# Phase 1 of a two-layer attention kernel: split float32r products in place of Strassen's seven

## The chip, the cores and the metric

The kernel runs on one core of one Trainium2 chip. The time is device microseconds for the whole kernel, from one launch. An "image" below is one of the eight entries of the batch.

## The reference

Two attention layers follow each other on x of shape (8, 512, 32, 32), that is 8 images of 512 channels and T = 1024 tokens. Only the first layer's projections matter here:

```
h   = group_norm(x)                       # 32 groups of 16 channels
qkv = einsum('oc,bct->bot', qkv_w, h) + qkv_b     # 1536 outputs from 512 channels
q, k, v = per head, fake_quant(each)      # needs min and max of all q, of all k, of all v
w   = softmax(q^T k * scale);  a = v w;  x = x + proj_w a + proj_b
# layer 1: group norm, q, k, v, softmax attention with one head, projection, residual
```

fake_quant uses the minimum and maximum over the whole tensor, so no score can be computed before all eight images have their q, k and v. This divides the kernel in two phases.

## The kernel before

**Phase 1** (the block that opens the pools p1w, p1, p1o and ps_1) computes q, k and v of all images, keeps running maxima and minima in columns of `rcs` and stores the raw values in DRAM (`q_d`, `k_d`, `v_d`). Then `ext`, `exa` and `scl` reduce the extremes to the three scales, and **phase 2** loads q, k and v, quantizes them and computes both attention layers. It takes the rest of the time, and the change leaves its code as it is.

In phase 1 the 512 channels lie on 128 partitions in CC = 4 chunks, and the 1024 tokens in two halves of 512. Three images of x are held (`p1`, tag x), loaded by `load_x` on SyncE's DMA queue. `norm_steps` takes statistics on VectorE, averages them over groups with two small matmuls on TensorE (`gps`, `gps2`), and scales x in place on VectorE.

Products are in full fp32. `qk_block(b, j)` computes q and k of a pair of heads for all tokens as one 2x2 by 2x2 block product with Strassen's seven products; `v_block(b, n)` does the same for v. The sums that Strassen needs are made on VectorE: `weight_sums` once, `token_sums` for each image. Each product is two accumulating matmuls of 512 columns (q, k) or four of 256 (v). `keep` copies intermediate sums out of PSUM on ScalarE, `add_max` adds and takes the maximum on VectorE, `store` takes the minimum and starts the DMA. For image 0, four of the twelve tiles of rows (q and k of the first pair) are plain fp32 products, because these can start as soon as a chunk of x is normed.

The order is written out by hand. Every block is a generator that yields after each product; the list TURNS says whose product is next, and a step of `ahead` (`prepare(b + 1)`, the next image's norm and token sums) is taken after every other product. `mm` keeps the matmuls in this order on TensorE. VectorE's instructions in phase 1 are put in order by the framework.

`l1p` is a pool whose tags (h, v, g, rs, rs1, acc1) are shared with phase 2's tiles. `load_folded` loads weights for phase 2 into tags h and v, on ScalarE's DMA queue.

Of the kernel before, what the change touches and what calls it, by code (L numbers as in the profile page):

```python
# [9 lines left out]
F32 = mybir.dt.float32  # L10
BF = mybir.dt.bfloat16
# [19 lines left out]
SM1 = 1.0 / math.sqrt(C)  # L31

# [21 lines left out]
def attn_pair_kernel(  # L54
# [145 lines left out]
    def mm(ps, lhsT, rhs, **kw):  # L200
        ins = nc.tensor.matmul(ps, lhsT=lhsT, rhs=rhs, **kw).ins  # L201
        part = lhsT.shape[-1] / P if lhsT.shape[-1] in (32, 64) else 1.0
        if rhs.dtype in (BF, F16):
            part *= 0.25 * lhsT.shape[0] / P
        pe.t += math.prod(rhs.shape[1:]) * 1.677e-3 * part
        if last_mm[0] is not None:
            tc.add_manual_dep(ins, last_mm[0].name, IN_ORDER, reason="order")
        last_mm[0] = ins
# [11 lines left out]
    def norm_steps(  # L220
        src, dst, wcol, bank, nm, ccs=range(CC), fine=False, put=None, mv=None
# [36 lines left out]
        )  # L258
        for hf in range(NH):
            for i, cc in enumerate(ccs):  # L260
                put(hf, 0.5, lambda i=i, cc=cc, hf=hf: dve.tensor_scalar(
                    dst(cc, hf), src(cc, hf), mean[:, i : i + 1], rstd[:, i : i + 1],
                    ALU.subtract, ALU.mult,
                ))
                if fine and i % 2 == 1:
                    yield
# [3 lines left out]
    def group_norm(src, dst, wcol, bank, nm):  # L270
        for _ in norm_steps(src, dst, wcol, bank, nm):
# [4 lines left out]
    q_d = [[dram.tile([P, T], F32, tag=f"q{b}_{j}", name=f"q_d{b}_{j}") for j in range(PAIRS)]  # L276
           for b in range(B)]
    k_d = [[dram.tile([P, T], F32, tag=f"k{b}_{j}", name=f"k_d{b}_{j}") for j in range(PAIRS)]
           for b in range(B)]
# [9 lines left out]
    with ExitStack() as fast:  # L289
# [84 lines left out]
        with tc.tile_pool(name="p1w", bufs=1) as p1w, tc.tile_pool(name="p1", bufs=3) as p1, tc.tile_pool(  # L374
            name="p1o", bufs=4
        ) as p1o, tc.tile_pool(name="ps_1", bufs=8, space=PSUM) as ps_1:
# [4 lines left out]
            wqkv = p1w.tile([P, CC, 3 * C], F32, name="wqkv")  # L381
            wn = {}
            xs, hs, cs = {}, {}, {}
            col = {n: 0 for n in ("qmax", "kmax", "vmax", "vmin")}

            def column(name, tile_):
                col[name] += 1
                return tile_[:, col[name] - 1 : col[name]]
# [7 lines left out]

            def load_x(b):
                xs[b] = p1.tile([P, CC, T], F32, tag="x", name=f"x1_{b}")
                for cc in range(CC):
                    nc.sync.dma_start(xs[b][:, cc, :], x_v[b, :, cc, :])  # L400
                    if b == 0:
                        nc.sync.dma_start(wqkv[:, cc, 0:C], w_qkv[:, cc, 0:C])

            def norm(b, parts=1, fine=False):

                hs[b] = xt = xs.pop(b)
                n = CC // parts
                return [
# [3 lines left out]
                        V_GN0W, one, f"a{b}_{i}", range(i * n, (i + 1) * n), fine,  # L412
                    )
                    for i in range(parts)
                ]

            K0, K1 = slice(0, CC // 2), slice(CC // 2, CC)

            room = l1p.tile([P, 6, 512], F32, tag="g", name="room")
            vs = room[:, 0:4, :].rearrange("p s (k n) -> p s k n", k=CC // 2)
            wa_flat = wa.rearrange("p s k n -> p (s k n)")
            ss = [
                wa_flat[:, i * 1024 : (i + 1) * 1024].rearrange("p (k n) -> p k n", k=CC // 2)
                for i in range(3)
            ] + [room[:, 4:6, :]]

            def tt_behind(*args):
                dve.tensor_tensor(*args)  # L430
                dve.after(normed)

            def weight_sums():
                tt = tt_behind
                (a11, a12), (a21, a22) = (
                    [wqkv[:, k, bass.ts(i, C)] for k in (K0, K1)] for i in (0, 1)
                )
                tt(ss[0], a21, a22, ALU.add)
                yield
                tt(ss[1], ss[0], a11, ALU.subtract)  # L440
                yield
                tt(ss[2], a11, a21, ALU.subtract)
                yield
                tt(ss[3], a12, ss[1], ALU.subtract)
                yield
                (w11, w12), (w21, w22) = (
                    [wqkv[:, k, 2 * C + i * C // 2 : 2 * C + (i + 1) * C // 2] for i in (0, 1)]
                    for k in (K0, K1)
                )
                tt(vs[:, 0], w11, w12, ALU.subtract)  # L450
                yield
                tt(vs[:, 1], w22, vs[:, 0], ALU.subtract)
                yield
                tt(vs[:, 2], w22, w12, ALU.add)
                yield
                tt(vs[:, 3], w21, vs[:, 1], ALU.subtract)
                yield

            def quarters(b):
                h = hs[b]  # L460
                return [h[:, k, bass.ts(hf, 512)] for k in (K0, K1) for hf in range(NH)]

            def token_sums(b):
                a, b_, c, d = quarters(b)
                cs[b] = t = l1p.tile(
                    [P, 4, CC // 2, 512], F32, tag="hv"[b % 2], name=f"sums_{b}"
                )
                tt = dve.tensor_tensor if b else tt_behind
                tt(t[:, 0], b_, a, ALU.subtract)
                yield  # L470
                tt(t[:, 1], d, t[:, 0], ALU.subtract)
                yield
                tt(t[:, 2], d, b_, ALU.subtract)
                yield
                tt(t[:, 3], c, t[:, 1], ALU.subtract)
                yield

            def prepare(b):
                yield from norm(b, fine=True)[0]
                yield from token_sums(b)  # L480

            def add_max(dst, ps, other, mx):
                dve.tensor_tensor_reduce(
                    dst, ps, other, 1.0, -3.0e38, ALU.add, ALU.max, accum_out=mx
                )

            def qk_block(b, j):

                a, _, c, d = quarters(b)
                t1, t2, t3, t4 = (cs[b][:, i] for i in range(4))  # L490
                a11, a12, a22 = wqkv[:, K0, 0:C], wqkv[:, K1, 0:C], wqkv[:, K1, C : 2 * C]
                s1, s2, s3, s4 = ss
                x, y = (one(f"qkps_{b}_{j}_{i}") for i in range(2))
                u = p1o.tile([P, 2, 512], F32, tag="u", bufs=2, name=f"u_{b}_{j}")
                u4 = p1o.tile([P, 512], F32, tag="u4", bufs=1, name=f"u4_{b}_{j}")
                q = p1o.tile([P, T], F32, tag="qk", name=f"q1_{b}_{j}")
                k = p1o.tile([P, T], F32, tag="qk", name=f"k1_{b}_{j}")
                bq, bk = qkb[:, j : j + 1], qkb[:, PAIRS + j : PAIRS + j + 1]

                def product(ps, w, r, start):  # L500
                    for i in range(CC // 2):
                        mm(
                            ps, lhsT=w[:, i, bass.ts(j, P)], rhs=r[:, i, :],
                            start=start and i == 0, stop=(i == CC // 2 - 1), skip_group_check=True,
                        )

                def keep(dst, bias):
                    act.activation(dst, x, AF.Identity, bias=bias)

                def store(t, mn, dst):  # L510
                    dve.tensor_reduce(
                        mn[:, b * PAIRS + j : b * PAIRS + j + 1], t, AX.X, ALU.min
                    )
                    nc.sync.dma_start(dst[b][j], t)

                product(x, a11, a, True)
                keep(u[:, 0, :], bq)
                yield
                product(y, a12, c, True)
                add_max(q[:, 0:512], y, u[:, 0, :], column("qmax", qmax))  # L520
                yield
                product(x, s2, t2, False)
                keep(u[:, 1, :], bk)
                yield
                product(y, s3, t3, True)
                yield
                product(x, s1, t1, False)
                keep(u4, bk)
                add_max(k[:, 512:T], y, u4, column("kmax", kmax))
                yield  # L530
                product(x, s4, d, False)
                dve.tensor_scalar(
                    q[:, 512:T], x, bq, None, ALU.add, ALU.max, accum_out=column("qmax", qmax)
                )
                store(q, qmin, q_d)
                yield
                product(y, a22, t4, False)
                add_max(k[:, 0:512], y, u[:, 1, :], column("kmax", kmax))
                store(k, kmin, k_d)
                yield  # L540

            def v_block(b, n):

                a, _, c, d = quarters(b)
# [1499 lines left out]
```

## Time and profile before

| | |
|---|---|
| median of 3 runs | 2645.51 us (2643.5 to 2645.55) |
| span of the profiled execution | 2641.2 us (no other time of that execution is given) |
| phase 1's last Strassen matmul ends | about 611.6 us into the span |
| TensorE busy in the span | 2585.6 us (98%) |
| VectorE busy | 1880.1 us (71%) |
| ScalarE busy | 1256.9 us (48%) |
| DMA, mean over the span | 92 GB/s |

PE is TensorE's matmul records, PEld its weight loads, which run beside them, DVE is VectorE, ACT ScalarE, POOL GpSimd, SP SyncE. A line such as `L201 PE MATMUL out<-in 128*128 128x512 f32 x8` is eight records, stationary tile 128*128, moving operand 128x512. Groups list busy time, mean ns of one record, and the engine's idle time ahead of it with its releaser. Matmul records are longer than their spacing, since they overlap.

### The profile page before, as it was taken

What the parts mean: (1) busy time and instruction counts of PE and PEld (TensorE: products, weight loads), DVE (VectorE), ACT (ScalarE), POOL (GpSimd) and SP (SyncE); (2) the same over time, 40 slices, a digit from 0 to 9 for tenths busy, and PEclk for the clock granted to TensorE, in tenths of its full rate; (3) what the DMA queues carried; (4) which work ended last, traced back from release to release, by engine and by line L of the source; (5) the groups of instructions that cost most, each with busy time, mean ns of one, the idle gap of its engine ahead of it and who ended that gap; (6) DMA issues with size and microseconds to landing.
All of it is one profiled execution on the core that took longest, in us unless ns stands there. A gap on an engine that the chain in (4) does not pass through costs nothing.

```text
span 2641.2 us, 33393 instructions
## 1 busy us (share of the span) xinstructions
PE 2585.6 (98%) x13150; PEld 1657.2 (63%) x13150; DVE 1880.1 (71%) x2733; ACT 1256.9 (48%) x1582; POOL 195.7 (7%) x157
## 2 busy tenths in 40 slices
PE   8999999998998999999999999999999999999998
PEld 4655555553235775766577567757665775677687
DVE  7766666658777777877777677778777776776544
ACT  0011111115866664666566566646665665664121
POOL 0000000001110001000100010011001000100000
PEclk9999999999999999999999999999999999999999
DMA  5233322234321132223222321322232123212211
GB/s 203 112 128 112 127 99 101 88 119 152 134 67 41 57 104 89 85 66 110 94 61 77 112 89 57 105 88 85 64 111 95 61 77 112 89 38 79 100 37 38
DMA packets 146887, 241.96 MB, mean 92 GB/s; under 512 B 26528, under 2 KB 92064, under 8 KB 145184
## 3 DMA queue, kind: packets, MB, share of 16 engines
q1 hardware_dynamic: 115872, 181.50, 20.5%
q10 hardware_dynamic: 30848, 58.23, 6.5%
q8 instruction: 105, 1.72, 0.3%
q14 instruction: 62, 0.51, 0.1%
HBM read 152.86 MB, written 86.28 MB: 91 GB/s over the span
## 4 chain that ended last, share of the span: by engine, by line
PE 83%; DVE 8%; ACT 3%; issue 2%; DMA 2%; POOL 1%; SPq 0%; ACTq 0%; DVEq 0%; POOLq 0%
PE s L201 15%; PE qkps L201 13%; PE o L201 12%; PE pj L201 8%; PE av L201 7%; PE v2ps L201 7%; PE vps L201 6%; PE g L201 5%; PE st L201 4%; PE sm L201 4%; ACT pt L86 2%; DVE two L86 1%; DVE sums L86 1%; DVE x L86 1%; DMA out_dram<-x 1%
## 5 line engine op out<-in xcount | busy, mean ns | idle before, releaser
L86 DVE TENSOR_TENSOR two<-pt,two 128x1024 f16<-128x1024 f32 x496 | 596.7, 1219 | 143.6 <-POOL two L909 114.1
L86 ACT ACTIVATE pt<-st,esc 128x1024 f32<-128x1024 f32 x496 | 527.0, 1116 | 355.3 <-PE st L201 335.5
L86 ACT CAST two<-pt 128x1024 f16<-128x1024 f32 x358 | 362.3, 1056 | 8.4 <-issue 5.8
L86 ACT ACTIVATE u<-qkps,qkb 128x512 f32<-128x512 f32 x90 | 61.9, 687 | 500.5 <-PE qkps L201 500.5
L909 POOL CAST two<-pt 128x1024 f16<-128x1024 f32 x128 | 171.0, 1336 | 1553.6 <-PE sm L201 1028.1
L201 PE MATMUL av<-two,v 128*64 128x512 f16 x1984 | 246.0, 383 | 0.0
L201 PE MATMUL s<-g,h 128*128 128x256 f32 x1024 | 234.1, 381 | 0.0
L201 PE MATMUL pj<-ao,wp 128*128 128x512 f32 x512 | 223.6, 595 | 0.0
L201 PEld LDWEIGHTS s<-g,h 128*128 128x128 f32 x1024 | 192.8, 190 | 31.9 <-issue 4.3
L201 PE MATMUL st<-q,k 64*128 64x512 bf16 x1024 | 162.0, 382 | 21.5 <-ACT pt L86 11.9
L201 PEld LDWEIGHTS <-v 128*64 128x64 f16 x1984 | 98.1, 109 | 133.5 <-issue 65.6
L201 PE MATMUL s<-g,sums 128*128 128x256 f32 x768 | 178.4, 381 | 0.2 <-DVE p L86 0.2
L201 PE MATMUL o<-p,v 128*128 128x256 f32 x768 | 175.2, 382 | 1.0 <-DVE p L86 1.0
L201 PEld LDWEIGHTS pj<-ao,wp 128*128 128x128 f32 x512 | 96.1, 190 | 121.3 <-issue 112.7
L201 PE MATMUL qkps<-sums,wa 128*128 128x512 f32 x360 | 164.6, 592 | 0.0
L201 PEld LDWEIGHTS o<-p,v 128*128 128x128 f32 x768 | 144.3, 190 | 27.1 <-issue 5.7
L201 PEld LDWEIGHTS s<-g,sums 128*128 128x128 f32 x768 | 144.7, 190 | 24.2 <-issue 4.1
L201 PE MATMUL qkps<-x,wqkv 128*128 128x512 f32 x304 | 141.1, 603 | 0.8 <-DVE x L86 0.8
L201 PE MATMUL sm<-two,ones 128*32 128x512 f16 x1984 | 137.7, 383 | 0.5 <-ACT rs L86 0.5
L201 PE MATMUL g<-h,wa 128*128 128x256 f32 x512 | 121.7, 386 | 2.1 <-DVE h L86 2.1
L201 PEld LDWEIGHTS <-k 64*128 64x128 bf16 x1024 | 33.9, 94 | 141.6 <-issue 139.1
L201 PE MATMUL v2ps<-wm,h 128*128 128x256 f32 x512 | 119.9, 383 | 0.7
(202 smaller groups left out, 3566.9 us busy)
## 6 DMA issues: line engine op xcount, KB each, us to landing
rs<-rs_d SPq DMA_DIRECT2D x80, 256.0 KB
x<-in_x_dram SPq DMA_DIRECT2D x32, 512.0 KB
raw<-q_d SPq DMA_DIRECT2D x32, 512.0 KB
raw<-k_d SPq DMA_DIRECT2D x32, 512.0 KB
v_d<-v SPq DMA_DIRECT2D x32, 512.0 KB
x_d<-h SPq DMA_DIRECT2D x64, 256.0 KB
x<-x_d ACTq DMA_DIRECT2D x64, 256.0 KB
out_dram<-x SPq DMA_DIRECT2D x64, 256.0 KB
```

The lines of the kernel that those rows point to most:

```text
L86: ins = self.latest = op(*args, **kw).ins
L201: ins = nc.tensor.matmul(ps, lhsT=lhsT, rhs=rhs, **kw).ins
L909: copy(two[:, 0], pt)
```

## The change

Phase 1 no longer uses Strassen's scheme. Each fp32 operand is split into a high and a low half of 12 bits each, both kept as float32r, and a third term `mix`. Of two split operands the four half products come out of three products: high by high and low by low are summed in one PSUM bank, a; the mixed term by the mixed term is summed in another, m; `put` combines the two with fixed factors.

- `split_weights` makes the three forms of the weights once (`wsp`: w_high, w_low, w_mix), in six chunks; `split_half(b, hf)` makes them for one half of one image's tokens. The high part and the scaled low part of the weights are made on ScalarE, low and mix on VectorE.
- `three` issues 8 matmuls into a and 4 into m for each 128x512 tile of output; for v a ninth matmul (`pick`, `vrow`) adds the bias into a.
- `put` copies a to SBUF on ScalarE with scale and bias (`u_ring`), then adds m on VectorE and takes the maximum. `store` takes the minimum over two tiles and starts one DMA of 512 KB.
- `apply` scales x by the norm on ScalarE, one instruction for each channel chunk, except for image 0.
- x lies in the tags h and v of `l1p` (two images), the split halves in p1 (two), q's and k's output in `out_ring` (the memory of wa, three tiles), v's in `v_ring` (three tiles).
- q and k lie in DRAM by two pairs of heads (`q_two`, `k_two`); q_d and k_d are views of these.
- Image 0 still computes q and k of its first pair in full fp32.
- The order is by halves: all blocks of the first token half of an image, then all of the second. Beside the blocks go the steps of `side`: in the first half the split of the image's second half and the norm of the next image, in the second half the next image's first split. `load_x(b + 2)` is issued at the start of the second half, `load_folded("v", ...)` in the last image's second half.

The core of the diff:

```diff
+            def split_weights(g, cs):
+                high, low, mix = (t[:, g, cs] for t in wsp)
+                act.activation(high, raw_w[:, g, cs], AF.Identity, scale=NUDGE)
+                dve.tensor_tensor(low, raw_w[:, g, cs], high.bitcast(F32), ALU.subtract)
+                dve.after(normed)
+                dve.scalar_tensor_tensor(
+                    mix, low.bitcast(F32), -SH, high.bitcast(F32), ALU.mult, ALU.add
+                )
+                dve.after(normed)
+                act.activation(low, low.bitcast(F32), AF.Identity, scale=SH)
+
+            def split_half(b, hf):
+                halves[b, hf] = t = p1.tile(
+                    [P, 3, CC, 512], F32R, tag="half", name=f"half_{b}_{hf}"
+                )
+                for k in (slice(0, CC // 2), slice(CC // 2, CC)):
+                    high, low, mix = (t[:, i, k, :] for i in range(3))
+                    src = xs[b][:, k, bass.ts(hf, 512)]
+                    act.activation(high, src, AF.Identity, scale=NUDGE)
+                    yield
+                    dve.tensor_tensor(low, src, high.bitcast(F32), ALU.subtract)
...
+                    dve.scalar_tensor_tensor(
+                        mix, low.bitcast(F32), -SH, high.bitcast(F32), ALU.mult, ALU.add
+                    )
...
+            def three(nm, left, right, first=None):
+                a, m = (one(f"{nm}_{i}") for i in range(2))
+                pairs = [(left[i][cc], right[i][cc]) for i in range(2) for cc in range(CC)]
+                if first is not None:
+                    pairs.insert(0, first)
+                for i, (lt, rt) in enumerate(pairs):
+                    mm(a, lhsT=lt, rhs=rt, start=(i == 0), stop=(i == len(pairs) - 1))
+                for cc in range(CC):
+                    mm(m, lhsT=left[2][cc], rhs=right[2][cc], start=(cc == 0), stop=(cc == CC - 1))
+                return a, m
+
+            def put(dst, a, m, bias, name):
+                i = turn_of("u", 3)
+                u = u_ring[:, i, :] if i < 2 else u_last
+                act.activation(u, a, AF.Identity, bias=bias, scale=-(SH + 1.0))
                 dve.tensor_tensor_reduce(
+                    dst, m, u, -1.0 / SH, -3.0e38, ALU.add, ALU.max, accum_out=column(name)
+                )
+
+            def store(t, name, dst):
+                dve.tensor_reduce(column(name), t, AX.XY, ALU.min)
+                nc.sync.dma_start(dst, t)
...
-            TURNS = (0, 0, 2, 0, 0, 2, 0, 2, 0, 0, 2, 1, 1, 2, 1, 1, 2, 1, 2, 1, 1)
...
+            for b in range(B):
+                for hf in range(NH):
+                    if hf == 0:
+                        ahead = norm(b + 1, fine=True)[0] if b + 1 < B else iter(())
+                        if b == 0:
+                            side = [more, more, ahead]
+                        else:
+                            side = [split_half(b, 1), ahead]
...
+                    for _ in blocks(b, hf):
+                        for g in side:
+                            go(g)
+                        n += 1
+                        if hf == 1 and b + 1 < B and n == (4 if b else 3):
+                            for _ in ahead:
+                                pass
+                            side = [split_half(b + 1, 0)]
```

For image 0, `more` is the first half's split, the six chunks of weights and the second half's split in turn.

## The prediction

> **What bounds the kernel now.** I start with the page's busy times, to see which engine could set the end, and then look at the change's own stage, phase 1, with busy time by stretch. The stretches begin where the timeline of TensorE (PE) shows the first Strassen block (51.83), the start of image 1 (about 99.8), image 7 (538.4) and the end of phase 1 (611.6).
> ```profile
> PE 2585.6 (98%) x13150; PEld 1657.2 (63%) x13150; DVE 1880.1 (71%) x2733; ACT 1256.9 (48%) x1582; POOL 195.7 (7%) x157
> 52.00:99.80 47.80, 47.80 (x169) 31.62 (x169) 38.50 (x80) 4.12 (x6) 1.02 (x1) 1.00 0.19 74
> 99.80:538.40 438.60, 437.68 (x1371) 257.89 (x1371) 287.82 (x565) 49.49 (x72) 6.05 (x6) 1.00 0.29 111
> 538.40:611.60 73.20, 73.13 (x227) 42.59 (x225) 39.08 (x79) 8.24 (x12) 0.00 (x0) 1.00 0.31 118
> ```
> After the stretch and its length come busy us of PE, PEld, DVE, ACT, POOL, then granted clock and DMA share. PE is busy for all but 1 us in 438.6, at full clock; VectorE (DVE) 66%, ScalarE (ACT) 11%. Busy alone isn't peak, so I check the cadence: in the chain of waits the same piece recurs once per image.
> ```profile
> 128.72 3.40 DVE sums L86 x3
> ...
> 201.82 3.40 DVE sums L86 x3
> ...
> 274.93 3.40 DVE sums L86 x3
> ```
> The period is 73.1 us. The timeline of 330 to 345 us shows what fills it:
> ```profile
> 331.85 1.89 PE L201 MATMUL vps<-room,sums 128*128 128x256 f32 x8
> 331.85 1.49 PEld L201 LDWEIGHTS vps<-room,sums 128*128 128x128 f32 x7 [0.24 <-issue]
> 333.57 1.88 PE L201 MATMUL qkps<-x,room 128*128 128x512 f32 x4
> ```
> Every fp32 matmul leaves two records (high and low part of the weights), so four matmuls are eight records. Eight of 256 columns take 333.57 - 331.85 = 1.72 us, 0.215 each; in the chain eight of 512 columns take 3.43, 0.429 each. An image has 4x14 matmuls of 512 columns and 2x7x4 of 256: 112 x 0.429 + 112 x 0.215 = 72.1 us of the 73.1. So PE streaming is the bound here, and the 1.0 left is the group norm's two small matmuls and rare waits.
>
> **What the Trainium skill says.** "TensorE: Matmul & The Clock Gate", section "Wait — 56ns, not 53.3ns?", gives N/2.4 GHz + 2.5 ns for a warm one-pass matmul, 216 ns at 512 columns. The same page, "LDWEIGHTS (loading the stationary operand)", prices a load by its 128 columns, an estimate of 107 ns; the records here are 190. "Perfetto Trace Analysis", section "Engine Utilization", halves the output rate for fp32's low/high form. The trace agrees: 256 columns twice in 0.215, 512 twice in 0.429. Its step ① ("Step-by-step: what each phase is for", first page) has loads pulled ahead of running matmuls: the seven loads above follow every 0.215 us, with no time added though each lasts 0.19. No page gives a speed for float32r.
>
> **PE's part.** A Strassen block goes; each output tile of 128x512 becomes 8 matmuls into a and 4 into m, with one more for v's bias. An image has 8 q, 8 k and 8 v tiles: 24 x 12 + 8 = 296 matmuls. Were float32r to stream one column per cycle, each would last 0.2155 (the page's 216, and the trace's 0.215 for equally long streams with equal loads): 63.8 us, against 72.1. The matmul is bounded below by that streaming. From above: were nothing hidden, 0.19 + 0.215 = 0.405; were float32r run like fp32, 0.86. I take the low end, because a 0.19 load under a 0.215 stream is what v's records show. With the same 0.9 for the norm an image is 64.7 us, 8.4 less than 73.1.
>
> **The vector engine's part** must stay below 64.7. Durations, from groups by shape within 99.8 to 611.6:
> ```profile
> L86 DVE CUSTOM_DVE_ANT_0 v<-vps,uv 128x512 f32<-128x512 f32 x43 | 29.6, 688 | 42.6 <-PE vps L201 42.3
> L86 DVE TENSOR_REDUCE rcs<-v 128x1 f32<-128x1024 f32 x29 | 35.3, 1219 | 0.8
> L86 DVE BATCH_NORM_STATS2 gst_a<-x 128x6 f32<-128x512 f32 x40 | 25.8, 678 | 8.5 <-DMA x<-in_x_dram 8.2
> L86 DVE TENSOR_TENSOR sums<-x,sums 128x1024 f32<-128x1024 f32 x12 | 14.6, 1220 | 0.0
> L86 ACT ACTIVATE u<-qkps,qkb 128x512 f32<-128x512 f32 x84 | 57.7, 687 | 456.6 <-PE qkps L201 456.6
> ```
> Per image: 24 put (0.69 plus 0.08 accumulator read) 18.5; 12 minima 14.6; 8 statistics 5.4, 4 aggregates 0.8 and the small norm steps 1.2; four low of split_half at 1.22, 4.9; four mix. No immediate-scalar operation of mix's kind and size is shown; between 1.22 (as a tensor_tensor) and 1.42 (as ao's, 1416 ns with a pointer scalar) I take 1.3: 5.2. Sum 50.6 us, 78% of 64.7. The normalization leaves DVE for ACT.
>
> ACT: 24 x 0.69 for u, four high and four apply at about 1.1 (the exp of 128x1024 is 1116 ns): 16.5 + 8.9 = 25.4, under 40%. Both costs lie beside PE.
>
> **DMA and order.** Bytes are unchanged: 2 MB in, 6 MB out an image. The 12 stores stay 12 of 512 KB; q's and k's rows become 2 KB. 8.4 MB in 64.7 us is 130 GB/s, where the page's first slice moved 203. An x load now starts only when split_half(b, 1) has read that buffer, about mid-image, and the statistics need it half an image later: about 30 us for 2 MB; at 130 GB/s beside the stores it needs 16. SP's queue holds stores behind those loads; three-deep rings give a store over 10 us, so I cost it zero; without cover it would show as DVE waiting on q_d stores. load_folded("v") moves half an image forward on ACT's queue: two 1 MB issues, some 1.5 us of ACTq; no gain counted.
>
> **What gets a new wait.** In the first half of images 1 to 6 the norm's matmuls stand in PE's order, behind which every later tile is queued. They wait for statistics that share DVE with put and split_half. Over the first five tiles (13 us of PE) DVE has 5 x 0.77 + 2 x 1.22 + 1.22 x 2 + 1.3 + 6.2 = 16.2, so up to about 3 us of lag, or nothing if the statistics run ahead. They do run ahead in the old trace: fold_room, written after the whole loop, runs at 600.99 between phase 1's own evictions, so DVE's order follows readiness. I take 1.0 per image.
>
> **Image 0** keeps its 16 matmuls of q and k in full fp32 and must also split the weights. Its remaining PE work is 8 x 12 x 0.2155 + 8 x 13 x 0.2155 = 43.1 us, where 51.83 to 100.49 was 48.7: 5.6 gained at best. But DVE from 26.4 us has six weight chunks (2.52 each, 15.1), three half splits (5.04 each, 15.1), 8 evictions (6.7), 12 minima (14.6), the norm (7.4), 16 put (12.3) and about 2 for v's bias: 73 us by durations. In the old timeline 1.22-long records start every 1.13 (26.39, 27.53, 28.66), so some 100 of them overlap by 0.08 each: about 65 us net, for the 68 until 94.8. That is nearly full, so I leave only 1.5 of the 5.6.
>
> **Sum.** Image 0: 1.5; images 1 to 6: 6 x (8.4 - 1.0) = 44.4; image 7 without a norm: 8.4. Together 54.3. The end of phase 1 (last tile, minimum, partition reduction) is as long as before, and phase 2 is unchanged: zero, within 2 either way as its start shifts. The profiled span is 2641.2; no separate time of that execution is shown, and the median of the runs, 2645.5, lies 4.3 above it. 2641.2 - 54.3 + 4.3 = 2591.2.
>
> **Rivals.**
> (1) The weight load or the stream of float32r costs more than 0.244 us a matmul: (73.1 - 0.9)/296 is where the gain ends. For it: the trace has no float32r, and the margin is 13%. At 0.405 an image is 120.8 and the kernel 8 x 47 = 376 slower, 3020; run as fp32, worse (some 3700). If float32r isn't one pass the change doesn't do what it says, and it ends here too. Against: the 256-column cadence. Chance 0.10.
> (2) DVE lag becomes PE's wait: 3 us in six images and no gain in image 0 leave 6 x 5.4 + 8.4 = 41, less 3 for a late split: 38, 2607. For: 16.2 in 13 us. Against: readiness order. Chance 0.22.
> (3) Everything hides: 5.6 + 7 x 8.4 = 64, 2581. Chance 0.17.
> (4) Waits of several kinds (ring, x load, splits at image borders) eat nearly all of it: within 0.2%, 5 us, which is about what a measurement can tell. Chance 0.03.
> The forecast itself: 0.48. Faster 0.87, same 0.03, slower 0.10.
>
> The range reaches from (3), with 3 us for phase 2's start, to a little past (2): 2578 to 2614.
>
> **What would show it.** Right: chain pieces recurring every 64.7 to 66 us from image 1 on; float32r matmuls 0.215 apart, with loads of 0.19 or less; DVE near 50 us and ACT near 25 an image. Wrong: PE waiting for put, gmv or half; a cadence above 0.23; image 1 starting after 100.

## The result, and the profile after

| | before | after |
|---|---|---|
| median, four runs each on one chip | 2644.51 us (2643.45 to 2645.55) | 2626.16 us (2624.79 to 2630.44) |
| span of the profiled execution | 2641.2 us | 2623.2 us |
| image 1's first product starts | 100.49 us | 110.22 us |
| phase 1's last product ends | 611.6 us | 591.5 us |

The ratio is 0.9934, 95% interval 0.9920 to 0.9948: faster, by 18 us where 54 were forecast. The time lies 12 us above the upper end of the range, 2614. The two spans differ by 18.0 us, so the profiles can be set against each other in place of the medians. The start of image 1 before, which the prediction names without its line:

```profile
100.49 2.74 PE L201 MATMUL qkps<-x,wqkv 128*128 128x512 f32 x6
```

First the busy times of the page after, then busy time by stretch; the three stretches are the split part of image 0, images 1 to 6, and image 7. After the stretch and its length come PE, PEld, DVE, ACT, POOL, the granted clock and the DMA share.

```profile
PE 2556.4 (97%) x13686; PEld 1755.6 (67%) x13686; DVE 1864.0 (71%) x2675; ACT 1390.1 (53%) x1750; POOL 193.4 (7%) x160
```

```profile
54.30:110.20 55.90, 49.04 (x206) 39.43 (x205) 45.05 (x85) 21.17 (x27) 1.02 (x1) 0.94 0.37 132
110.20:522.70 412.50, 412.00 (x1800) 335.76 (x1799) 268.39 (x510) 143.72 (x192) 6.06 (x6) 1.00 0.34 123
522.70:591.50 68.80, 68.76 (x299) 55.67 (x297) 38.44 (x78) 17.95 (x27) 0.00 (x0) 1.00 0.32 123
```

In images 1 to 6 PE is busy for all but 0.5 of 412.5 us, at full clock. VectorE needs 268.4/6 = 44.7 us an image and ScalarE 24.0, both far below the 68.75 that PE takes. So PE's stream is still the bound there. In image 0 it isn't: PE stands idle for 6.86 of 55.9 us, and the granted clock is 0.94.

The chain of waits of the kernel after shows the image's period and its pieces (start, length, what, number of instructions):

```profile
317.21 11.00 PE qkps L206 x48
328.21 3.03 PE vps L206 x13
...
334.61 11.11 PE qkps L206 x48
...
403.29 11.11 PE qkps L206 x48
```

From 334.61 to 403.29 the period is 68.68 us, against 73.1 before. (The 0.11 above 11.00 is the norm's small matmul ahead of these pieces.) Four q or k tiles are 48 matmuls in 11.00 us, **0.2292 us each**; a v tile is 13 in 3.03, **0.2331**. The prediction had 0.2155.

The terms beside PE, from groups by shape within 100 to 590 us (busy time and mean ns after the bar):

```profile
L206 PEld LDWEIGHTS qkps<-half,w_high 128*128 128x128 f32 x448 | 83.7, 188 | 18.2
L91 DVE SCALAR_TENSOR_TENSOR half<-half 128x1024 fp32r<-128x1024 f32 x26 | 31.7, 1221 | 0.0
L91 ACT ACTIVATE x<-x,goff_a,grstd_a 128x1024 f32<-128x1024 f32 x24 | 28.4, 1234 | 1.2 <-DVE goff_a L91 1.0
L91 ACT ACTIVATE half<-x 128x1024 fp32r<-128x1024 f32 x26 | 26.1, 1053 | 4.3 <-PE vps L206 4.3
```

Loads last 188 ns and are hidden. `mix` takes 1.22 us (forecast 1.3), `apply` 1.23 and `high` 1.05 (both about 1.1).

Image 0 is where time is lost outright. PE's timeline of the kernel after, with the idle time ahead of an entry and its releaser in brackets:

```profile
67.85 1.10 PE L206 MATMUL vps<-w_mix,half 128*128 128x512 f32 x4
75.81 0.56 PE L206 MATMUL gps_a<-gmv_a,gavg 128*128 128x4 f32 x2 [6.86 <-DVE gmv_a L91]
76.23 0.77 PE L206 MATMUL vps<-vrow,pick 128*128 128x512 f32 x1
76.80 1.91 PE L206 MATMUL vps<-w_high,half 128*128 128x512 f32 x4
78.51 1.54 PE L206 MATMUL vps<-w_low,half 128*128 128x512 f32 x4
...
80.82 0.28 PE L206 MATMUL gps_a<-gd_a,gavg 128*128 128x4 f32 x2
```

The matmul that waits is the group average of image 1's norm. It stands in PE's order between two v tiles of image 0, and these wait behind it though all they need is there. What VectorE does meanwhile, from its own timeline, and below it the busy times of two stretches, most of the wait and what follows it:

```profile
67.20 0.20 DVE L91 BATCH_NORM_AGGREGATE gmv_a<-gst_a 128x2 f32<-128x12 f32 x1
67.31 0.64 DVE L91 CUSTOM_DVE_ANT_0 wa<-qkps,u_last 128x512 f32<-128x512 f32 x1
...
67.87 1.22 DVE L91 SCALAR_TENSOR_TENSOR half<-half 128x1024 fp32r<-128x1024 f32 x1
69.01 1.28 DVE L91 BATCH_NORM_STATS2 gst_a<-x 128x6 f32<-128x512 f32 x2
...
70.92 1.18 DVE L91 TENSOR_TENSOR half<-x,half 128x1024 fp32r<-128x1024 f32 x1
...
74.34 1.21 DVE L91 TENSOR_REDUCE rcs<-wa 128x1 f32<-128x1024 f32 x1
75.46 0.20 DVE L91 BATCH_NORM_AGGREGATE gmv_a<-gst_a 128x2 f32<-128x12 f32 x1
```

```profile
70.50:75.80 5.30, 0.00 (x0) 0.02 (x1) 5.30 (x10) 0.00 (x0) 0.00 (x0) 0.70 0.72 220
76.30:79.20 2.90, 2.90 (x8) 2.32 (x8) 2.70 (x9) 0.00 (x0) 0.00 (x0) 0.50 1.00 407
```

VectorE works for all 5.30 us of the first stretch, in which PE does nothing. The statistics share it with low and mix of the second half's split, `put` and the minimum, and the last `gmv_a` comes at 75.46; PE follows at 75.81. After the wait the granted clock is 0.50 for some us: the four `w_high` matmuls take 78.51 - 76.80 = 1.71 us, where 0.93 is usual, and this v tile takes 80.82 - 76.23 = 4.59 where 3.03 is usual.

### The profile page after: what moved, and what is told of

Same layout as the page of the kernel before. It is cut to its first block, busy times and chain, and to the rows that moved or that the text cites. A ratio compares the mean times of both kernels' runs of the same rounds, so it can differ in the third digit from the quotient of the medians.

```text
span 2623.2 us, 34796 instructions
## 1 busy us (share of the span) xinstructions
PE 2556.4 (97%) x13686; PEld 1755.6 (67%) x13686; DVE 1864.0 (71%) x2675; ACT 1390.1 (53%) x1750; POOL 193.4 (7%) x160
## 4 chain that ended last, share of the span: by engine, by line
PE 87%; DVE 6%; issue 2%; ACT 2%; DMA 2%; POOL 0%; ACTq 0%; SPq 0%; DVEq 0%; POOLq 0%
PE s L206 15%; PE o L206 14%; PE qkps L206 13%; PE pj L206 8%; PE av L206 8%; PE v2ps L206 7%; PE vps L206 7%; PE g L206 7%; PE st L206 4%; PE sm L206 4%; DVE two L91 1%; ACT pt L91 1%; DMA raw<-q_d 1%; PE fold L206 0%; DVE acc L91 0%
## 5 line engine op out<-in xcount | busy, mean ns | idle before, releaser
L91 ACT ACTIVATE u_ring<-qkps,qkbt 128x512 f32<-128x512 f32 x89 | 60.9, 685 | 140.9 <-PE qkps L206 131.2
L206 PE MATMUL qkps<-half,w_high 128*128 128x512 f32 x480 | 130.5, 394 | 0.0
L206 PE MATMUL qkps<-half,w_mix 128*128 128x512 f32 x480 | 129.5, 392 | 0.0
L206 PE MATMUL qkps<-half,w_low 128*128 128x512 f32 x480 | 129.4, 391 | 0.0
```

The lines of the kernel that those rows point to most:

```text
L91: ins = self.latest = op(*args, **kw).ins
```

## The experiments

My theory had two parts. (a) A float32r matmul streams more slowly than one of 2-byte operands, in every image. (b) Image 0 loses by order, a norm matmul that is queued behind a full VectorE. Against (a) stood a fixed cost for each matmul, and the weight load; against (b), that image 0 is short of VectorE time in any order.

**Shorter streams.** To part a cost per column from one per matmul, q's tiles are computed in pieces of 384 and 128 columns and k's in two of 256; v stays at 512.

```diff
+                w = {"q": 384, "k": 256}.get(nm[0], 512)
+                for lo in range(0, 512, w):
+                    cs = slice(lo, min(lo + w, 512))
                     for i, (lt, rt) in enumerate(pairs):
-                        mm(a, lhsT=lt, rhs=rt, start=(i == 0), ...)
+                        mm(a[:, cs], lhsT=lt, rhs=rt[:, cs], start=(i == 0 and lo == 0), ...)
...
```

> Cadence of float32r matmuls by width: every q product is issued as 384 and then 128 columns, every k product as 256 and 256, v stays at 512 (same output, more matmuls). Theory A (a fixed cost of some 16 ns on each float32r matmul[...]): 0.176 us at 384 columns, 0.123 at 256. Theory B (the stream itself is slower, 0.229/512 = 0.447 ns a column): 0.172 at 384 and 0.115 at 256, or 0.12 if the load then bounds it. Theory C (the weight load sets the spacing): 0.229 at every width.

It took 2666.89 us (one run). PE's timeline of this kernel:

```profile
325.17 0.64 PE L206 MATMUL kps<-half,w_low 128*128 128x256 f32 x4
325.64 1.10 PE L206 MATMUL kps<-half,w_mix 128*128 128x256 f32 x8
326.58 0.63 PE L206 MATMUL kps<-half,w_high 128*128 128x256 f32 x4
...
335.47 0.86 PE L206 MATMUL qps<-half,w_high 128*128 128x384 f32 x4
336.17 0.85 PE L206 MATMUL qps<-half,w_low 128*128 128x384 f32 x4
336.86 0.56 PE L206 MATMUL qps<-half,w_high 128*128 128x128 f32 x4
337.26 0.61 PE L206 MATMUL qps<-half,w_low 128*128 128x128 f32 x4
```

Starts, not lengths, give the cadence. Eight of 256 columns: 326.58 - 325.64 = 0.94, 0.1175 each. Eight of 384: 336.86 - 335.47 = 1.39, 0.1737 each. With 0.2292 at 512 the steps are 0.0562 and 0.0555 for 128 columns each, a straight line of about 0.436 ns a column with 6 ns on top. The 2-byte rate, from the next run's 0.2158 less the 2.5 ns that the Trainium skill's page "TensorE: Matmul & The Clock Gate" (section "Wait — 56ns, not 53.3ns?") puts on top of the columns, is 0.417 ns a column. So by this estimate most of the extra (0.019 x 512 = 10 ns of 13.4) goes with the columns and 3 to 4 ns with the matmul. And 0.1175 lies well below a load's 188 ns record, so the load's record length doesn't set the cadence. At 128 columns something else begins to count: 337.26 - 336.86 is 0.40 for four, 0.10 each, where the line would give 0.062. The kernel has no such streams.

**2-byte operands.** The same schedule with every split operand in bf16.

```diff
-            wsp = [p1w.tile([P, CC, 3 * C], F32R, name=f"w_{n}") for n in ("high", "low", "mix")]
+            wsp = [p1w.tile([P, CC, 3 * C], BF, name=f"w_{n}") for n in ("high", "low", "mix")]
...
-                    [P, 3, CC, 512], F32R, tag="half", name=f"half_{b}_{hf}"
+                    [P, 3, CC, 512], BF, tag="half", name=f"half_{b}_{hf}"
```

> All operands of the split products are bf16 in place of float32r (the halves lose bits, so the output is only approximate; same instructions and order). If the extra 0.0137 us a matmul belongs to the 4-byte float32r operands: 0.2155 us spacing for q and k, an image at 64.7 us. If it belongs to the order of the matmuls, their PSUM use or the load of new weights each time: 0.229 as before.

It took 2595.09 us (one run), 31 less than the change. Its chain of waits:

```profile
401.18 10.36 PE qkps L206 x48
411.54 5.61 PE vps L206 x26
```

48 in 10.36 are 0.2158 each, 26 in 5.61 the same. The forecast's cadence was that of 2-byte operands, q, k and v alike; what is dearer comes with the float32r operands. The run doesn't part the moving operand from the load, since its loads are shorter too (98 ns for 188). The granted clock is 1.00 in images 1 to 6 of both kernels, so no lower clock that the traces show explains it. At this cadence the norm's matmuls do wait for VectorE (3.1 us over five `gd_a` entries), which under the slower stream was hidden but for 0.50 us.

**The same two streams at half clock.** Two runs show this beside their own purpose: in this kernel and in the one with v's bias on VectorE (below) a long idle of PE in image 0 (7.72 and 6.25 us) is followed by a stretch at half clock. Busy time by stretch, first bf16, then float32r (the granted clock is the third column from the end):

```profile
75.20:80.20 5.00, 5.00 (x13) 1.93 (x12) 3.88 (x10) 0.60 (x1) 0.00 (x0) 0.50 0.57 232
```

```profile
73.50:78.70 5.20, 5.20 (x14) 4.04 (x13) 4.13 (x12) 0.00 (x0) 0.00 (x0) 0.50 0.63 254
```

PE's timelines of the two in these stretches, in the same order:

```profile
76.83 1.91 PE L206 MATMUL vps<-w_low,half 128*128 128x512 bf16 x4
78.54 1.91 PE L206 MATMUL vps<-w_mix,half 128*128 128x512 bf16 x4
```

```profile
75.28 1.91 PE L206 MATMUL vps<-w_low,half 128*128 128x512 f32 x4
76.99 1.91 PE L206 MATMUL vps<-w_mix,half 128*128 128x512 f32 x4
```

From start to start both take 1.71 us for four, 0.4275 each. At half clock float32r cost nothing extra. If it took more cycles of PE's clock, the extra would have doubled. Argued, not shown, is what limits it: this fits a limit on something that feeds 4-byte operands at a rate of its own, reached at full clock alone. Which feed it is (moving operand, load, or their sum) no run here shows.

**The norm of image 1 later.** In image 0's first half the step `ahead` is left out, so the norm's matmuls come in the second half, with the same work in all.

```diff
-                            side = [more, more, ahead]
+                            side = [more, more]
```

> The norm of image 1 moves from the first half of image 0 to its second half, past the splitting of the weights. Theory order (TensorE's 6.9 us wait at the norm's matmul is only where that matmul stands in the queue): the wait goes, the clock isn't lowered by it either, image 1 starts 6 to 9 us earlier, the kernel is 6 to 9 us faster than the change (about 2618). Theory capacity (VectorE has too much to do in image 0 whatever the order): the wait comes back at the second half's split or at image 1's first split, gain 0 to 2 us.

2618.46 us (2617.95 to 2620.61), ratio 0.9899 [0.9882, 0.9915]: 7.7 less than the change. PE's timeline:

```profile
84.52 0.28 PE L206 MATMUL gps_a<-gmv_a,gavg 128*128 128x4 f32 x2
86.83 0.39 PE L206 MATMUL gps_a<-gd_a,gavg 128*128 128x4 f32 x2 [2.03 <-DVE gd_a L91]
...
102.02 1.09 PE L206 MATMUL qkps<-half,w_high 128*128 128x512 f32 x4
```

The 6.86 is gone, 2.03 remain, and between 14 and 110 us the granted clock is 1.00. Image 1 starts at 102.02 instead of 110.22; 1.6 of these 8.2 are an earlier first product (14.49 for 16.11). VectorE has nearly as much to do in less time (from 14 us to the start of image 1 it is busy for 74.4 of 88.0 us, where it was 77.2 of 96.2 in the change), so it was the order that cost, as theory (b) has it. The gain is still there when phase 1 ends, at 583.3 for 591.5. After it the profiled execution took 3.8 us longer (2035.5 us for the rest, 2031.7 in the change); the change once more, below, bears on these.

**Less work on VectorE, same order.** The minima of image 0's q, k and v are left out (their columns set to 0), about 14.6 us of VectorE.

```diff
+                if image[0] == 0:
+                    dve.memset(column(name), 0.0)
+                else:
+                    dve.tensor_reduce(column(name), t, AX.XY, ALU.min)
```

> The changed kernel with image 0's twelve minima left out (their columns are set to 0 instead, so the minima are those of seven images): 12 x 1.13 us less on VectorE, the order unchanged. If the 6.9 us wait at the norm's matmul is VectorE's backlog, the six minima that come before it (6.8 us) take nearly all of it away, and image 1 starts 6 to 9 us earlier. If the wait has another cause (x(1) landing late, ScalarE's queue), it stays within 2 us.

2618.02 us (one run), 8.1 less than the change. The same matmul and the start of image 1 on PE's timeline:

```profile
68.70 0.36 PE L206 MATMUL gps_a<-gmv_a,gavg 128*128 128x4 f32 x2 [1.11 <-DVE gmv_a L91]
...
101.42 1.09 PE L206 MATMUL qkps<-half,w_high 128*128 128x512 f32 x4
```

6.86 became 1.11, and image 1 starts 8.8 us earlier, 1.4 of which are an earlier first product (14.76 for 16.11). With the order kept, a shorter backlog does nearly the same as a later matmul: the wait is order times backlog, and either one removes it.

**v's bias off PE.** The ninth matmul of a v tile goes; the bias is added by VectorE where the other tiles' is added by ScalarE.

```diff
-                act.activation(u, a, AF.Identity, bias=bias, scale=-(SH + 1.0))
+                if bias is None:
+                    dve.scalar_tensor_tensor(u, a, -(SH + 1.0), vrow, ALU.mult, ALU.add)
+                else:
+                    act.activation(u, a, AF.Identity, bias=bias, scale=-(SH + 1.0))
...
-                        (pick, vrow),
```

> v's bias is no longer a ninth matmul into a; VectorE adds it where ScalarE copied a out. If TensorE's stream sets phase 1 (my theory): 64 matmuls fewer at 0.233 us, 14.9 us less, about 2611. If VectorE is close to a bound in all images (rival): its 64 x 0.75 us = 48 us more cost as much as they save, no gain; only in image 0, where VectorE is full, I expect 2 to 5 us given back.

2613.55 us (2612.45 to 2614.67), ratio 0.9882 [0.9866, 0.9899]: 12.6 less than the change. 64 matmuls of 0.233 are 14.9. From its chain of waits:

```profile
359.46 11.01 PE qkps L206 x48
370.47 5.60 PE vps L206 x24
376.07 11.20 PE qkps L206 x48
```

A v tile still has 0.2333 a matmul (5.60/24), so the ninth matmul isn't why v is dearer than q and k. And here ten of the q and k pieces, the first at 140.93 and the last at 443.32, take about 11.20, 0.2333 too, for 11.00 elsewhere, 2.0 us in all. In images 1 to 7 the gain is 10.9 us (470.4 for 481.3) where 56 matmuls less are 13.1, so this is nearly all that is missing. What decides between 0.2292 and 0.2333 stays open. PE waits 0.4 us in all in these images, so the added work on VectorE (0.69 us for each v tile) is hidden there.

**Both together.**

> Both edits together: the norm of image 1 in the second half of image 0, and v's bias added on VectorE in place of a ninth matmul. If TensorE's queue sets phase 1, the gains add up: 7.7 and 12.6 us off the change, about 2606, ratio 0.9854. If the freed TensorE time only uncovers VectorE in image 0 (12 us more of additions over all images, 12 of them in image 0), 3 to 6 us of that come back, about 2610.

2611.31 us (2609.22 to 2614.13), ratio 0.9874 [0.9859, 0.9889]. It beats both given kernels, but can't be told from the last one: of the 7.7 us of the later norm about 2 are left. On PE's timeline the two waits for the norm in image 0 are 1.01 and 1.11 us, so that wait went as it should. Two losses take its place, a stretch at half clock behind these waits and waits for VectorE's split at the start of image 1:

```profile
88.00:91.40 3.40, 3.40 (x10) 2.63 (x9) 2.46 (x7) 2.17 (x3) 0.07 (x1) 0.50 0.00 0
```

```profile
104.59 0.73 PE L206 MATMUL qkps<-half,w_low 128*128 128x512 f32 x2 [0.82 <-DVE half L91]
...
106.85 0.74 PE L206 MATMUL qkps<-half,w_mix 128*128 128x512 f32 x2 [1.07 <-DVE half L91]
```

VectorE is busy for 70.3 of the 75.8 us from 26.4 to image 1's start, and PE waits 1.9 us for it. So the rival to (b), too little VectorE time, does show once the order is mended and VectorE has the bias to add as well. (The expectation's "12 us more" is misreckoned: 64 additions of 0.69 us are 44 us in all, 5.5 of them in image 0.) Phase 1 ends at about 575.0 where it ended at 577.5 with v's bias alone, and the rest takes 2035.2.

**The change once more**, beside the last two, to see how steady its start is.

> The changed kernel once more, unaltered, for a closer interval beside the others: 2626 us, ratio 0.993. GpSimd's first power began at 14.0 us in the changed kernel's profile, at 11.1 in the old one's and at 12.4 to 12.8 in four variants: if this start varies from run to run, the first matmul of this profile will stand anywhere from 13 to 16 us; if the change causes it, at 16.

2626.9 us (2622.8 to 2630.1), ratio 0.9932 [0.9919, 0.9946]. The wait is 6.86 us again. The first product starts at 15.36, where it was 16.11 in the first profile, and the `first_pow` on GpSimd ahead of it at 13.26, where it was 14.01: the start moves by some us between executions and kernels, so not all of the 2.8 us by which the change started late is the change's.

The rest after phase 1 moves too: 2034.3 us here (the last product ends at 590.7), 2.6 more than in the first profile of the same kernel. Busy time and granted clock of the 215 us after phase 1, for the change, the change once more and the later norm:

```profile
591.50:806.50 215.00, 187.69 (x1078) 68.91 (x1080) 166.84 (x223) 150.71 (x170) 32.55 (x24) 0.98 0.29 94
590.70:805.70 215.00, 189.04 (x1069) 68.81 (x1068) 165.61 (x224) 149.47 (x168) 30.79 (x24) 0.96 0.29 94
583.30:798.30 215.00, 188.50 (x1055) 68.27 (x1056) 165.56 (x218) 149.41 (x168) 30.28 (x24) 0.95 0.29 94
```

The clock is 0.98 where the rest takes 2031.7, 0.96 where it takes 2034.3, and 0.95 where it takes 2035.5; with both edits it is 0.95 and 2035.2. So the 3.8 and 3.5 us that those two variants lost after phase 1 go with the clock, and since the unaltered kernel moves by 2.6 they can't be charged to the edits. Why the clock falls there in some executions isn't shown.

## Why the prediction was off

In the spans, 54.3 us were forecast and 18.0 came. The 36.3 missing are 23.0 in images 1 to 7 (52.8 forecast; 511.1 us before, 481.3 after, so 29.8), 11.2 in image 0 (a gain of 1.5 forecast, a loss of 9.7 found) and 2.1 after phase 1.

- **"Were float32r to stream one column per cycle"** is the step that failed. The mechanism held: one pass a matmul, 296 an image, loads hidden, PE the bound. But 0.2155 was the low end of an unknown, carried over from fp32 matmuls of 256 columns, which are as long but not the same operand form. Measured: 0.2292 for q and k, 0.2331 for v. An image then costs 192 x 0.0137 + 104 x 0.0176 = 4.5 us more, 31 in seven. The bf16 run took 27.8 off these images (453.5 us for 481.3), with 3.1 us of waits come back in them. The skill's 216 ns ("TensorE: Matmul & The Clock Gate", section "Wait — 56ns, not 53.3ns?") agrees with bf16's 0.2158 here; for float32r the measurement decides. The text said that no page gives float32r a speed, and still put its range on the low end: 7% on this one term was worth 31 us, and no part of that was in the forecast or in the range's upper end, which came from rival (2). Only rival (1) named such a cost, from 0.244 on. Between 0.2155 and 0.244 there was no case, and the sign of being wrong, "a cadence above 0.23", lay too high: 0.2292 passes under it and cost 2.6 us an image.
- **"I take 1.0 per image"** for the norm's wait: it came to at most 0.5 in six images together. That gives 5.5 back. The slower stream hides it; at bf16's cadence a part returned. What is left of images 1 to 7 is the small norm matmuls, which fill less than the 0.9 allowed. The wait's reason was another as well. The one wait, with what stands ahead of it on three engines' timelines, in image 3 (from 247.59):

```profile
253.93 0.34 SPq L420 DMA_DIRECT2D x<-in_x_dram  x1
262.59 1.29 DVE L91 BATCH_NORM_STATS2 gst_a<-x 128x6 f32<-128x512 f32 x2 [1.20 <-DMA x<-in_x_dram]
265.53 0.39 PE L206 MATMUL gps_a<-gd_a,gavg 128*128 128x4 f32 x2 [0.50 <-DVE gd_a L91]
```

The sixth load of x starts at 253.93, that of image 5, so the statistics run a whole image ahead, and on VectorE they stand between the steps of image 4's norm. VectorE stood idle for x, not behind in its work (4.5 us at seven places in images 1 to 7). In the bf16 run the chain leads from each of the five waits back to such a load. So the 30 us of slack that the prediction gave a load of x weren't there.
- **"So I leave only 1.5 of the 5.6"** in image 0: the sum of VectorE's work was right in kind, and with the norm later it fitted but for 2.03 us of waiting; that it was "nearly full" the run with both edits shows. The step left out order. The wait of a norm matmul in PE's queue was costed for images 1 to 6 and not for image 0, where the list of side steps has the same `ahead` and VectorE is fullest. Split products began 2.5 us later than in the kernel before (54.30 for 51.83). From there to image 1 the 55.9 us are 8.7 above the forecast's 47.2 (48.7 - 1.5): 6.86 of waiting, 1.6 of half clock on the v tile behind it, and 3.1 of cadence (96 x 0.0137 + 104 x 0.0176), less the 4.1 held back of the gain, plus about 1.2 of norm matmuls and short stretches. The skill's page has the clock as well: its section "What's actually happening" states that an idle window of about 3.4 us halves it. The trace agrees, 0.50 after 6.86 us, and none of this was in the sum. The length of one wait doesn't decide alone, though: 2.03 us in the run with the later norm left the clock at 1.00, and 1.01 and 1.11 us close together in the run with both edits were followed by 3.4 us at 0.50.
- **The end of phase 1 and phase 2, zero within 2:** 2.1 lost, about what was allowed. The change once more lost 2.6 more there and two variants 3.8 and 3.5, with the clock.
- **VectorE and ScalarE:** 44.7 and 24.0 us an image for 50.6 and 25.4. As in image 0 of the old trace, records that overlap by 0.08 make the sum of durations too high. The rings never held PE in images 1 to 7, and a load of x did so for 0.50 us.
- **Rival (2)**, 2607, lay nearer than the forecast, but by luck and for another reason: VectorE's lag became PE's wait in image 0 alone, the one image where rival (2) counted no more than a lost gain.
- **Two readings without weight in the result:** run like fp32, 2645 + 8 x (0.9 + 296 x 0.86 - 73.1) is about 4100, not 3700. And the halved rate for fp32 agrees with the trace for one record; a whole fp32 matmul of 512 columns leaves two of 0.429 us, four times bf16's 0.2158 in all.

## What to carry to other kernels

A matmul's cadence belongs to its operand form: take it from a row of that very form, or let the range hold both ends, since 7% of a term of some 490 us outweighs every wait in this case. Where one engine's instructions stand in a written order, ask for each that waits on another engine how long that engine's backlog is at that moment, in the first iteration above all, where one-time work is added. A wait that is taken away can come back on the next engine, as with both edits. And before a few us behind the changed stage are charged to an edit, compare the granted clock there, and the same kernel with itself.

## What was not expected of the hardware

- Float32r at full clock: 0.2292 to 0.2333 us for 512 columns, 0.1737 for 384, 0.1175 for 256, against 0.2158 for bf16 at 512. At half clock both take 0.4275.
- A PE idle of 6.86 us also cost about 1.6 us afterwards in matmuls at granted clock 0.50. Two waits of 1.01 and 1.11 us close together were followed by 3.4 us at 0.50 too, one of 2.03 us was not.
- The granted clock in the 215 us after phase 1 lay between 0.95 and 0.98, and differed between two executions of one kernel (0.98 and 0.96, 2.6 us).
- q's and k's matmuls, alike in shape and order, ran at 0.2292 in some stretches and 0.2333 in others of one kernel.
